# Two normalising multiplies of layer 0 on GpSimd, a third temporary in the back, and the first half's delta loads tied to one store

## The chip, the cores and the metric

The program runs on one core of one Trainium2 chip. The metric is the device time of one execution in microseconds (us), lower is better. The engines are called as in the profile: PE (TensorE), PEld (its weight loads), DVE (VectorE), ACT (ScalarE), POOL (GpSimd) and SP (SyncE, which issues the DMAs).

## The reference

Two layers act on an image of 2 x 96 x 96 x 96 (batch, channels, rows, columns). All of the change lies in layer 0. Cut to what matters:

```
x = x + L0_conv(_ln_c(x))          # _ln_c: norm over the channels, eps 1e-6
t = tokens(x);  t = t + L0_ffn(_ln_t(t));  x = image(t)
...layer 1...

def L0_conv(x):
    xin, z = split(in_proj(x));  z = silu(z)
    x_s = grid_sample_bilinear(xin, ref + offset(xin))      # 3x3 conv, norm, gelu, 1x1 conv, tanh
    # 512 windows of 6 x 6 tokens, 4 directions, 192 channels, 16 states
    delta = softplus(dt_proj(x_proj(x_s)) + bias)
    h[t] = h[t-1] * exp(delta * A) + delta * u * B[t]
    y[t] = sum over the 16 states of h[t] * C[t], plus D * u
    y = sum of the four directions
    y = (y - mean(y)) * rsqrt(var(y) + 1e-5) * ln_g + ln_b   # over the 192 channels
    return out_proj(y * z)
```

## The kernel before

Layer 0 walks 32 stripes (2 images x 16 stripes of 6 rows, T = 576 tokens, H2 = 288). A stripe has three parts, and the parts of neighbouring stripes overlap.

**Front** (`_l0_front`, L488). It norms x over the channels (`norm`, L532), projects, gates, convolves, samples bilinearly on POOL (`sample`, L675, 14 multiplies and adds), and for the two token orders o = 0, 1 computes B, C, delta and delta*u (`steps`, L781: four POOL operations in each of three channel groups m). The last step stores delta and delta*u in DRAM (`dl_d`, `du_d`; `store`, L825). Group m = 0 holds channels 0 to 127 of direction kk = 0, group m = 1 the same of kk = 1, and m = 2 the last 64 channels of both. In `norm`, ACT writes the square into `asq` and the centred value into `axc`; PE averages the square into PSUM tile `ava`; ACT makes it a reciprocal root in place (Ln, then Exp with -0.5, L548 and L549); DVE multiplies (L552). No GpSimd instruction of this kernel touches PSUM.

**Scan** (`_l0_scan`, `_l0_section`, L1055). A stripe has 64 units: half h of the channels (0, 1), order o, direction kk, quarter i of the states, half c of the tokens, in this nesting. A unit is: PE spreads B over 128 rows of PSUM (L1104, `bp`, two buffers), DVE multiplies by delta*u (L1108), ACT makes the decays (L1088, `dA`), DVE scans (L1125, result in one of six `h` buffers), POOL multiplies by C (L1130), PE adds up the states in PSUM tile `y` (L1143). The delta rows `dlr` and `dur` of a section (h, o, kk) come by one DMA each (L1073), two buffers each; before the change such a load is planned behind every store of its direction, m and m = 2. After 32 units ACT copies `y` into `Y` (L1039, L1041), of which there is one buffer.

**Back** (`_l0_back`, L936). It centres Y, norms it (`normed`, L971: PE averages the squares into `yva`, ACT makes the reciprocal root in PSUM, `_power`, L857; DVE multiplies both halves of Y, L975), multiplies by the gate z on POOL (L984), projects and adds the input (`pp`, L994 to L1001), and runs the feed-forward net (`_plan_ffn`). Its temporaries `ysq`, `ysq2`, `fxc`, `fsq` and `x2` share the buffers of tag "b", two before the change.

The order of the work is not written by hand. `_Plan` records every operation of all 32 stripes with its engine, a cost and a due time; `order` is a list scheduler that walks engines and buffers through these numbers, picks for each engine the operation that can start first, then the one due first, and takes a buffer only when one is free. What it gives is issued, and `_in_order` then fixes it: each of PE, DVE, ACT, POOL and SP executes its instructions in exactly that order. A cost that is a little longer or an edge less therefore gives another order everywhere. POOL's costs are 0.14 us + 0.0018 us a column (1.7 us for L1130). `keep` puts matmuls without use (L1188, on `minus`) where the plan leaves PE idle. A tile's `skip` leaves that many words free at its start.

Of the kernel before, what the change touches and what calls it, by code (L numbers as in the profile page):

```python
# [13 lines left out]
AF = mybir.ActivationFunctionType  # L14
ALU = mybir.AluOpType
# [11 lines left out]
C = 96  # L27
HW = 96
# [4 lines left out]
T = WIN * HW  # L33
H2 = T // 2
NS = 16
KG = 4
NQ = 4
CB = 32
NBL = C // CB
# [69 lines left out]
class _Plan:  # L109
# [19 lines left out]
    def op(self, eng, cost, run, r=(), w=(), due=0.0, tab=None, also=(), scan=False, first=False):  # L129
        o = _Op(eng, cost * self.rate.get(eng, 1.0), run, due, tab)  # L130
        o.scan, o.first = scan, first
        ref = lambda t: t if isinstance(t, tuple) else (t, None)
        meets = lambda a, b: a is None or b is None or a == b
        for t, key in map(ref, r):
            o.deps.update(p for p, q in t.writes if meets(key, q))
        for t, key in map(ref, w):
            o.deps.update(p for p, q in t.writes + t.reads if meets(key, q))
        for t, key in map(ref, r):
            t.reads.append((o, key))
        for t, key in map(ref, w):  # L140
            t.writes.append((o, key))
        o.deps.discard(o)
        for t in [x[0] for x in map(ref, list(r) + list(w))] + list(also):
            if t not in o.tiles:
                o.tiles.append(t)
        for t in o.tiles:
            if not t.users and t.tag != "p":
                t.queue.append(t)
            t.users.append(o)
        self.ops.append(o)  # L150
        return o
# [323 lines left out]
def _cost(S, eng, cols):  # L475

    fixed, each = (RATE if S.fine else LOOSE)[eng]
    return fixed + each * cols


def _op(S):
    def op(eng, n, run, r, w, also=(), tab=None, times=1):
        S.op(eng, times * _cost(S, eng, n), run, r, w, also=also, tab=tab)

    return op


def _l0_front(k, P, S, f, x, b, s, at):  # L488
# [3 lines left out]
    nc = k.nc  # L492
# [4 lines left out]
    temp = lambda shape, name, skip=0: S.tile(P.front, shape, "g", P.ng, name=name, skip=skip)  # L497
# [4 lines left out]
    def pe(cols, run, r, w, also=()):  # L502
        S.op("pe", _cost(S, "pe", cols), run, r, w, also=also)

    def act(cols, run, r, w, tab=None, times=1):
        S.op("act", times * _cost(S, "act", cols), run, r, w, tab=tab)

    def dve(cols, run, r, w):
        S.op("dve", _cost(S, "dve", cols), run, r, w)
# [17 lines left out]
    pool(8, lambda: nc.gpsimd.memset(xin.ap[:, :, :, 1 : HW + 3 : HW + 1], 0.0), (), (xin,))  # L527
    rows = lambda t, c: t.ap[:, 4 * c : 4 * c + 4, :].rearrange("p r w -> p (r w)")
    N4 = 4 * HW
    xc, sq, xn = temp([C, 8, HW], "axc"), temp([C, 8, HW], "asq"), temp([C, 8, HW], "xn")  # L530

    def norm(c):  # L532
        pc, va = ps("axc"), ps("ava")
        pe(N4, lambda: nc.tensor.matmul(
            pc.ap[:C, :N4], k.less_mean, rows(xt, c), start=True, stop=True), (xt,), (pc,), (xc,))

        def centred():
            nc.scalar.activation(rows(sq, c), pc.ap[:C, :N4], AF.Square)
            nc.scalar.copy(rows(xc, c), pc.ap[:C, :N4])

        act(N4, centred, (pc,), ((xc, c), (sq, c)), times=2)
        pe(N4, lambda: nc.tensor.matmul(
            va.ap[:C, :N4], k.mean96, rows(sq, c), start=True, stop=True),
            ((sq, c),), (va,), (xn,))

        def power():
            v = va.ap[:C, :N4]
            nc.scalar.activation(v, v, AF.Ln, bias=k.eps6[:C])  # L548
            nc.scalar.activation(v, v, AF.Exp, scale=-0.5)  # L549

        act(N4, power, (), (va,), tab="e", times=2)
        dve(N4, lambda: nc.vector.tensor_tensor(  # L552
            rows(xn, c), rows(xc, c), va.ap[:C, :N4], ALU.mult), ((xc, c), va), ((xn, c),))

    def project(half, c):
        pi, n = ps("pi"), PART[half]
# [7 lines left out]
    for c in range(2):  # L564
        norm(c)
# [26 lines left out]
    t = temp([128, NBL, H2], "t")  # L592
# [255 lines left out]
def _dues(S, n0, at):  # L848

    ops = S.ops[n0:]  # L850
    whole, sofar = sum(o.cost for o in ops), 0.0
    for o in ops:
        o.due = at(sofar / whole)
        sofar += o.cost


def _power(k, op, v, eps, out=None):  # L857

    v_ = lambda: v.ap[:C, :H2]

    def run():
        k.nc.scalar.activation(v_(), v_(), AF.Ln, bias=eps[:C])
        k.nc.scalar.activation(v_() if out is None else out.ap, v_(), AF.Exp, scale=-0.5)

    op("act", H2, run, (), (v,) if out is None else (v, out), tab="e", times=2)
# [70 lines left out]
def _l0_back(k, P, S, f, ffn, res, dst, at):  # L936

    nc = k.nc
    n0 = len(S.ops)
    Y, zs = f.Y, f.zs  # L940
    temp = lambda name: S.tile(P.back, [C, T], "b", 2, name=name)
    ps = lambda name: S.tile(P.ps, [128, 512], "p", P.np, name=name)
    cols = lambda c: slice(c * H2, (c + 1) * H2)

    op = _op(S)
    xr = S.tile(P.back, [C, T], "xr", 1)
    S.op("sp", 1.2, lambda: nc.sync.dma_start(
        xr.ap.rearrange("p (i w) -> p i w", w=HW), res), (), (xr,))
    x1, sq = xr, [temp("ysq"), temp("ysq2")]

    def both(w, src, name, r):

        out = ps(name)

        for half in range(2):
            op("pe", H2, lambda half=half: nc.tensor.matmul(
                out.ap[:C, :H2], w(half), src(half), start=(half == 0), stop=(half == 1)),
                r, (out,))
        return out

    def centred(c):
        pc = [both(lambda half, h=h: k.less_mean192 if half == h else k.minus_mean192,
                   lambda half: Y.ap[:, half, cols(c)], "yc", ((Y, c),)) for h in range(2)]
        for h in range(2):
            def run(h=h):
                nc.scalar.activation(sq[h].ap[:, cols(c)], pc[h].ap[:C, :H2], AF.Square)
                nc.scalar.copy(Y.ap[:, h, cols(c)], pc[h].ap[:C, :H2])

            op("act", H2, run, (pc[h],), ((sq[h], c), (Y, c)), times=2)

    def normed(c):  # L971
        va = both(lambda half: k.mean192, lambda half: sq[half].ap[:, cols(c)], "yva",
                  ((sq[0], c), (sq[1], c)))
        _power(k, op, va, k.eps5)
        op("dve", 2 * H2, lambda: nc.vector.tensor_tensor(  # L975
            Y.ap[:, :, cols(c)], Y.ap[:, :, cols(c)],
            va.ap[:C, :H2].unsqueeze(1).to_broadcast([C, 2, H2]), ALU.mult),
            (va,), ((Y, c),))

    for c in range(2):  # L980
        centred(c)
        normed(c)
    for h in range(2):
        op("pool", T, lambda h=h: nc.gpsimd.tensor_tensor(  # L984
            Y.ap[:, h], Y.ap[:, h], zs.ap[:, h], ALU.mult), (zs,), (Y,))

    def project(c):
        pp = ps("pp")

        half = slice(c * HW // 2, (c + 1) * HW // 2)  # L990
        img = lambda t: t.ap.rearrange("p (i w) -> p i w", w=HW)[:, :, half].rearrange(
            "p i (w j) -> p w i j", j=WIN)

        op("pe", H2, lambda: nc.tensor.matmul(  # L994
            pp.ap[:C, :H2], k.ident[:C, :C], img(x1), start=True, stop=False), (Y, zs, (x1, c)), (pp,))
        for n, (w, v) in enumerate(((k.w_outb, zs), (k.w_out, Y))):
            for h in range(2):
                op("pe", H2, lambda n=n, w=w, v=v, h=h: nc.tensor.matmul(
                    pp.ap[:C, :H2], w[:, h, :], v.ap[:, h, cols(c)],
                    start=False, stop=(n == 1 and h == 1)), (v,), (pp,))  # L1000
        op("act", H2, lambda: nc.scalar.copy(  # L1001
            img(x1), pp.ap[:C, :H2].rearrange("p (w i j) -> p w i j", i=WIN, j=WIN)),
            (pp,), ((x1, c),))

    for c in range(2):
        project(c)

    x2 = _plan_ffn(k, S, op, ps, temp, P.back, 1, ffn, x1)
    S.op("sp", 1.2, lambda: nc.sync.dma_start(dst, x2.ap), (x2,), ())
    _dues(S, n0, at)  # L1010
# [44 lines left out]
def _l0_section(k, P, S, f, first, o, h, kk, py, at, tau):  # L1055


    nc = k.nc
# [12 lines left out]
    for name, d in (("dlr", f.dl[kg]), ("dur", f.du[kg])):  # L1071
        t = S.tile(P.rep, [128, NBL, T], name, 2)
        S.op("sp", 2.6, lambda t=t, d=d: nc.sync.dma_start(  # L1073
            t.ap.rearrange("p b t -> p (b t)"),
            d.ap[:, 3 * h : 3 * h + 3, :].rearrange("c b t -> c (b t)").unsqueeze(1)
            .to_broadcast([CB, NQ, NBL * T])), (d,), (t,), due=at - 9 * tau)
        reps.append(t)
    dlr, dur = reps

# [961 lines left out]
```

## Time and profile before

| what | value |
|---|---|
| median of 3 runs (lowest, highest) | 8276.61 us (8267.24, 8282.14) |
| the profiled execution, and its span from first to last instruction | 8276.3 us, 8274.5 us |
| granted TensorE clock, mean | 0.959 |
| first scan starts, last scan ends | 149.4 us, 6227 us |
| busy between these two, of 6077.6 us: DVE, PE, POOL, ACT | 5896.2, 5297.0, 5019.1, 4695.2 us |
| L552, DVE: count, mean | 64, 532 ns |
| L975, DVE: count, mean | 64, 732 ns |
| L984, POOL, the nearest operation to those that move: count, mean | 64, 1203 ns |

A group of the profile is one line of code on one engine: busy time, mean length of one, then the time the engine sat idle just before such an instruction and who ended that idle time. A length runs from start to end of one instruction; neighbours on DVE overlap by a little, so spacing from start to start is shorter. The chain of work that ended last is the page's own account of the critical path; for this program it holds 28% of the span, so windows and waits say more.

### The profile page before, as it was taken

What the parts mean: (1) busy time and instruction counts of PE and PEld (TensorE: products, weight loads), DVE (VectorE), ACT (ScalarE), POOL (GpSimd) and SP (SyncE); (2) the same over time, 40 slices, a digit from 0 to 9 for tenths busy, and PEclk for the clock granted to TensorE, in tenths of its full rate; (3) what the DMA queues carried; (4) which work ended last, traced back from release to release, by engine and by line L of the source; (5) the groups of instructions that cost most, each with busy time, mean ns of one, the idle gap of its engine ahead of it and who ended that gap; (6) DMA issues with size and microseconds to landing.
All of it is one profiled execution on the core that took longest, in us unless ns stands there. A gap on an engine that the chain in (4) does not pass through costs nothing. (4 is left out here: it accounts for less than half of the span.)

```text
span 8274.5 us, 124621 instructions
## 1 busy us (share of the span) xinstructions
PE 7337.5 (89%) x46413; PEld 3261.5 (39%) x46413; DVE 7653.1 (92%) x5404; ACT 6308.6 (76%) x10654; POOL 5188.3 (63%) x3835
## 2 busy tenths in 40 slices
PE   7888888888888888888888888988878999989998
PEld 3333344434334333434443433433334223532245
DVE  3999999999999999999999999999996998969988
ACT  5777777778777887877777787778756886778867
POOL 4888888888888888888888888888862000110001
PEclk8999998999999999999999999999999999989999
DMA  3445544544545454454545454454441000110001
GB/s 93 159 156 156 157 151 155 156 151 156 157 153 158 156 166 153 153 159 155 155 150 157 150 157 156 155 159 158 154 132 47 3 3 20 33 47 3 2 22 33
DMA packets 359853, 992.25 MB, mean 120 GB/s; under 512 B 69288, under 2 KB 71680, under 8 KB 359040
## 3 DMA queue, kind: packets, MB, share of 16 engines
q1 hardware_dynamic: 357440, 984.04, 38.3%
q8 instruction: 367, 6.01, 0.3%
q14 instruction: 254, 2.08, 0.1%
q10 hardware_dynamic: 1792, 0.12, 0.0%
HBM read 797.19 MB, written 139.25 MB: 113 GB/s over the span
## 5 line engine op out<-in xcount | busy, mean ns | idle before, releaser
L1130 POOL TENSOR_TENSOR h<-h,cre 128x864 f32<-128x864 f32 x2048 | 3475.2, 1713 | 957.4 <-DVE h L1125 639.7
L1125 DVE TENSOR_TENSOR_SCAN h<-dA,bp 128x864 f32<-128x864 f32 x2048 | 3900.6, 1939 | 51.2 <-PE y L1143 30.6
L1088 ACT ACTIVATE dA<-dlr,A 128x576 f32<-128x576 f32 x3072 | 2157.9, 765 | 892.8 <-DVE h L1125 839.8
L1108 DVE TENSOR_TENSOR bp<-dur,bp 128x864 f32<-128x864 f32 x2048 | 2082.2, 1048 | 187.9 <-PE bp L1104 81.4
L1143 PE MATMUL y<-h,fold 128*32 128x288 f32 (+2 forms) x18432 | 1789.7, 436 | 229.6 <-POOL h L1130 202.1
L1143 PEld LDWEIGHTS y<-h,fold 128*32 128x32 f32 x18432 | 738.8, 114 | 963.4 <-POOL h L1130 674.8
L1503 ACT ACTIVATE pr<-sc 128x960 f32<-128x960 f32 (+1 forms) x1080 | 954.0, 937 | 200.1 <-PE sc L1499 179.2
L1104 PE MATMUL bp<-bt,selb 128*128 128x288 bf16 x2048 | 615.6, 301 | 508.4 <-DVE h L1125 491.2
L1583 DVE TENSOR_TENSOR sums<-sums,pr 128x3840 f32<-128x3840 f32 (+1 forms) x240 | 959.1, 3996 | 55.7 <-ACT pr L1503 33.7
L1675 POOL MEMSET vch<- 96x32 f32 x16 | 2.4, 153 | 1319.7 <-DVE dist L1537 1210.1
L1104 PEld LDWEIGHTS <-selb 128*128 128x128 bf16 x2048 | 198.9, 97 | 1200.9 <-DVE h L1125 1006.3
L1499 PE MATMUL sc<-qH,kH 32*128 32x480 f32 (+1 forms) x3240 | 627.4, 602 | 9.6 <-issue 5.0
L1188 PE MATMUL y<-selb,minus 128*32 128x288 bf16 x3528 | 605.7, 295 | 0.0
L1499 PE MATMUL sc<-q,kH 32*128 32x480 f32 (+1 forms) x1080 | 564.6, 602 | 0.0
L1565 PE MATMUL av<-pr,vT 128*32 128x480 f32 (+1 forms) x4320 | 533.4, 564 | 3.7 <-ACT av L1590 3.5
L1756 DVE SCALAR_TENSOR_TENSOR acc<-vch,lepe_w,acc 96x1152 f32<-96x1152 f32 x320 | 466.2, 1457 | 8.4 <-ACT vch L1691 0.4
L1188 PEld LDWEIGHTS <-minus 128*32 128x32 bf16 x3528 | 298.0, 98 | 225.6 <-issue 131.2
L1499 PEld LDWEIGHTS sc<-qH,kH 32*128 32x128 f32 x3240 | 219.6, 184 | 419.8 <-issue 220.6
L617 PE MATMUL pc<-xin,w_ca 128*128 128x288 f32 x1152 | 365.1, 423 | 1.2 <-ACT xin L560 1.2
L932 POOL TENSOR_TENSOR x<-x,fy 96x576 f32<-96x576 f32 x32 | 52.9, 1653 | 461.4 <-ACT fy L931 372.4
L791 PE MATMUL pt<-xd,w_dt 96*128 96x288 f32 x768 | 280.7, 455 | 7.3 <-ACT r L797 4.4
L810 POOL TENSOR_TENSOR e<-e,du 128x576 f32<-128x576 f32 x192 | 231.1, 1204 | 60.0 <-ACT du L806 59.7
(284 smaller groups left out, 10961.8 us busy)
## 6 DMA issues: line engine op xcount, KB each, us to landing
cre<-c_d SPq DMA_DIRECT2D x1024, 288.0 KB, 3.5
dur<-du_d SPq DMA_DIRECT2D x256, 864.0 KB, 5.6
dlr<-dl_d SPq DMA_DIRECT2D x256, 864.0 KB, 5.1
x<-xs SPq DMA_DIRECT2D x512, 72.0 KB, 2.4
du_d<-du SPq DMA_DIRECT2D x128, 288.0 KB, 2.5
dl_d<-dl SPq DMA_DIRECT2D x128, 288.0 KB, 2.6
du_d<-du SPq DMA_DIRECT2D x128, 144.0 KB, 2.5
dl_d<-dl SPq DMA_DIRECT2D x128, 144.0 KB, 2.4
```

The lines of the kernel that those rows point to most:

```text
L1088: nc.scalar.activation(dA.ap[:, :, blk, :], dlr.ap[:, blk, :].rearrange("p (c n) -> p c n", c=2), AF.Exp, scale=k.A[:, i, kg, h, blk : blk ...
L1104: nc.tensor.matmul(bp.ap[:, :H2], k.selb[:, kk, i, :], f.bc[o].ap[:, toks], start=True, stop=True)
L1108: nc.vector.tensor_tensor(bp.ap[:, : NBL * H2].rearrange("p (b n) -> p b n", b=NBL)[:, ::-1], dur.ap[:, ::-1, toks], bp.ap[:, :H2].unsquee ...
L1125: nc.vector.tensor_tensor_scan(hv, dv, bv, 0.0, ALU.mult, ALU.add)
L1130: nc.gpsimd.tensor_tensor(ht.ap, ht.ap, cre.ap[:, toks].unsqueeze(1).to_broadcast([128, NBL, H2]), ALU.mult)
L1143: nc.tensor.matmul(dst, k.fold, v, start=start, stop=stop)
L1188: nc.tensor.matmul(P.awake.ap[NBL * CB :, T - HEAD + 2 * 72 : HEAD], k.minus[:, :CB], k.selb[:, 0].rearrange("p i m -> p (i m)")[:, : HEAD ...
L1499: nc.tensor.matmul(two[to // 2][:, to % 2, :n], kH[rows, k0 : k0 + 128], q, start=True, stop=True)
L1503: nc.scalar.activation(pr[:, 2 * i : 2 * i + 2, :n], two[i][:, :, :n], AF.Exp, scale=HD**-0.5)
L1565: nc.tensor.matmul((main if s < HEADS else other)[s * HD : (s + 1) * HD, :n], vT[:, blk, hd, :], pr[:, place(s, p), :n], start=at == 0, st ...
L1583: nc.vector.tensor_tensor(both, both, pr[:, :, :, :n], ALU.add)
L1756: S.op("dve", 1.43, lambda: nc.vector.scalar_tensor_tensor(acc.ap, src(), W.lw[:, t : t + 1], acc.ap, ALU.mult, ALU.add), (vch,), (acc,))
```

## The change

Three edits, all in layer 0.

1. In the front's `norm` and in the back's `normed`, the reciprocal root is written by ACT into an SBUF tile (the tile of the squares, `asq` or `ysq`, which is free by then), and the multiply is POOL's and not DVE's. `asq` gets a skip of two words.
2. The back's shared temporaries get three buffers and not two, with a skip of two words.
3. For h = 0, the plan lets a load of `dlr` or `dur` follow the store of group m = kk alone. For h = 1 it stays behind all stores of its direction.

```diff
@@ _l0_front, norm
-    xc, sq, xn = temp([C, 8, HW], "axc"), temp([C, 8, HW], "asq"), temp([C, 8, HW], "xn")
+    xc, sq, xn = temp([C, 8, HW], "axc"), temp([C, 8, HW], "asq", 2), temp([C, 8, HW], "xn")
...
-            nc.scalar.activation(v, v, AF.Exp, scale=-0.5)
-
-        act(N4, power, (), (va,), tab="e", times=2)
-        dve(N4, lambda: nc.vector.tensor_tensor(
-            rows(xn, c), rows(xc, c), va.ap[:C, :N4], ALU.mult), ((xc, c), va), ((xn, c),))
+            nc.scalar.activation(rows(sq, c), v, AF.Exp, scale=-0.5)
+
+        act(N4, power, (), (va, (sq, c)), tab="e", times=2)
+        pool(N4, lambda: nc.gpsimd.tensor_tensor(
+            rows(xn, c), rows(xc, c), rows(sq, c), ALU.mult), ((xc, c), (sq, c)), ((xn, c),))
@@ _l0_back
-    temp = lambda name: S.tile(P.back, [C, T], "b", 2, name=name)
+    temp = lambda name: S.tile(P.back, [C, T], "b", 3, name=name, skip=2)
...
-        _power(k, op, va, k.eps5)
-        op("dve", 2 * H2, lambda: nc.vector.tensor_tensor(
+        rs = lambda: sq[0].ap[:, cols(c)]
+
+        def power():
+            nc.scalar.activation(va.ap[:C, :H2], va.ap[:C, :H2], AF.Ln, bias=k.eps5[:C])
+            nc.scalar.activation(rs(), va.ap[:C, :H2], AF.Exp, scale=-0.5)
+
+        op("act", H2, power, (), (va, (sq[0], c)), tab="e", times=2)
+        op("pool", 2 * H2, lambda: nc.gpsimd.tensor_tensor(
             Y.ap[:, :, cols(c)], Y.ap[:, :, cols(c)],
-            va.ap[:C, :H2].unsqueeze(1).to_broadcast([C, 2, H2]), ALU.mult),
-            (va,), ((Y, c),))
+            rs().unsqueeze(1).to_broadcast([C, 2, H2]), ALU.mult),
+            ((sq[0], c),), ((Y, c),))
@@ _l0_section, loads of dlr and dur
-            .to_broadcast([CB, NQ, NBL * T])), (d,), (t,), due=at - 9 * tau)
+            .to_broadcast([CB, NQ, NBL * T])), ((d, kk),) if h == 0 else (d,), (t,), due=at - 9 * tau)
```

In the built program every line after the second edit stands six lines lower (the scan L1125 becomes L1131, POOL's L1130 becomes L1136, the gate multiply L984 becomes L990, the loads L1073 become L1079); L552 keeps its number on its new engine, and L975 becomes L981.

## The prediction, made before the changed kernel ran

> **What bounds the kernel now.** I read the page's busy times and slices first, then the windows, then groups, waits and timelines of the part that is changed.
>
> ```profile
> PE 7337.5 (89%) x46413; PEld 3261.5 (39%) x46413; DVE 7653.1 (92%) x5404; ACT 6308.6 (76%) x10654; POOL 5188.3 (63%) x3835
> ...
> DVE  3999999999999999999999999999996998969988
> ...
> 149.40:6227.00 6077.60, 5297.01 (x34106) 2420.16 (x34105) 5896.23 (x4278) 4695.24 (x8118) 5019.07 (x3605) 0.96 0.49 154
> ```
>
> POOL works only in layer 0, so its 63% says little. The window (columns PE, PEld, DVE, ACT, POOL) runs from the first scan to the last: DVE is busy 5896.2 of 6077.6 us (97%), POOL 83%. DVE bounds this stage and stands idle for 181 us of it.
>
> ```profile
> 6204.37 2.03 DVE L1108 TENSOR_TENSOR bp<-dur,bp 128x864 f32<-128x864 f32 x2
> 6206.28 3.81 DVE L1125 TENSOR_TENSOR_SCAN h<-dA,bp 128x864 f32<-128x864 f32 x2
> 6209.99 2.03 DVE L1108 TENSOR_TENSOR bp<-dur,bp 128x864 f32<-128x864 f32 x2
> ```
>
> Undisturbed, two units take 6209.99 - 6204.37 = 5.62 us: each instruction costs less than its length, since neighbours overlap. So I price by spacing.
>
> ```profile
> L975 DVE TENSOR_TENSOR Y<-Y,yva 96x576 f32<-96x576 f32 x64 | 46.9, 732 | 10.2 <-ACT yva L863 10.2
> L552 DVE TENSOR_TENSOR xn<-axc,ava 96x384 f32<-96x384 f32 x64 | 33.8, 532 | 65.4 <-ACT ava L549 65.4
> ...
> DVE bp L1108 <- PE bp L1104: 81.4, 106, 2.6
> DVE h L1125 <- PE y L1143: 30.6, 26, 4.7
> DVE bp L1108 <- POOL h L1130: 27.8, 40, 1.9
> ```
>
> The last three are DVE's largest waits of the stage (total, times, longest): for PE's spread, and, twice over, for an `h` buffer that POOL or PE has not given back. Before the first scan it waits most:
>
> ```profile
> 133.43 1.37 SPq L1073 DMA_DIRECT2D dur<-du_d x2
> ...
> 147.22 4.10 ACT L1088 ACTIVATE dA<-dlr,A 128x576 f32<-128x576 f32 x6
> ...
> 138.80 2.03 DVE L1108 TENSOR_TENSOR bp<-dur,bp 128x864 f32<-128x864 f32 x2 [50.05 <-DMA dur<-du_d]
> 149.36 3.80 DVE L1125 TENSOR_TENSOR_SCAN h<-dA,bp 128x864 f32<-128x864 f32 x2 [8.54 <-ACT dA L1088]
> ```
>
> The first `dur` load leaves at 133.4 us, although group m = 0 was stored at 110.4; the stores of m = 2 (127.1 to 129.6) stand ahead of it.
>
> **What the Trainium skill says.** "GPSIMD Engine Reference", section 3.1, gives about 2.6 cycles an element for a two-input operation at 1.2 GHz: 1248 ns for 576 elements; the trace has L984 at 1203 and spacings of 1.28 us, so it agrees. "SBUF — State Buffer", section "Who interferes with whom", lets GpSimd and a DVE instruction with two SBUF inputs block each other. The stage's products and scans take one input from PSUM, and POOL's L1130 stays within 1702 and 1734 ns beside them: no block, here or for the two new operations. "ScalarE: Activation LUTs", section "Step-by-step: what each stage is for", calls PSUM the quicker destination: this trace has 387 ns for an Exp into PSUM (L863, `fva`) and 407 into SBUF (`frs`). "DMA: Bandwidth & Descriptors", section "Anatomy of one DMA", puts some 2 us of completion on a DMA; the stores here land 2.5 us after issue.
>
> **The change, part by part.** The sum is made against the profiled execution, 8276.3 us (span 8274.5); the median, 8276.61, is the same to 0.3 us, so nothing is shifted.
>
> *DVE gives up its multiplies.* L552: spacing 2001.55 to 2002.01 = 0.46 us, 60 of 64 within the stage (four come before the first scan): 27.6. L975: 1168.70 to 1169.35 = 0.65 us, 62 within (the last stripe's two come after the last scan): 40.3. Together **-67.9 us** on the engine that bounds the stage.
>
> *POOL takes them.* Neither is in the trace. From 576 to 864 columns the rows L984 and L1130 rise by 1713 - 1203 = 510 ns, 1.77 ns a column; so 384 columns take 1203 - 192 x 1.77 = 863 ns. Low end 0.80 (in proportion), high end 1.10 (in proportion to layer 1's slow L932, mean 1.65 us). L981, 576 columns: 1.28 by spacing, ends 1.20 and 1.65. I take 0.86 and 1.28: 2 x 0.86 + 2 x 1.28 = 4.3 us a stripe, 137 in all (128 to 176), queued ahead of L1130. POOL goes from 5019 to some 5155 of a stage of about 6020, 86%: cost nothing directly, hidden behind DVE's scans; uncovered it costs up to the 137.
>
> *Waits that grow.* (a) For `h` buffers, 30.6 + 27.8 = 58.4 us: priced over both built orders, POOL's other work between the h multiplies rises from 53.6 to 57.9 us a stripe, 8%; its longest run, 13 operations or 16.7 us, is the same, and there are 30 runs above 15 us in both. 8% of 58.4 is +5. (b) A moved multiply also gave PE half a microsecond more for the next spread. 106 of 1024 pairs of products wait for it, so 122 x 0.10 x 0.55 = +7. Together **+12**; ends -40 (the new order waits less) and +60.
>
> *The start.* In the changed order SP issues the loads of `dur` and `dlr` right after the m = 0 stores and one `c_d` store (112.9 in this trace). The wait for the store's landing holds SP to about 113.5; behind it stand the m = 1 stores (ready 115.5) and four `x` loads, which lose nothing. With 5.6 us to landing, `dur` is there at 119. Next late is ACT: its first decays stand behind the Relu of the next delta step (ends 126.3) and two `xin` copies, whose matmuls end at 128.1. So decays from 128.6, three of them 2.1 us, first scan at 130.8 instead of 149.4: -18.6. Two first norms on POOL add 0.3: **-18.3**. The next loads keep pace: kk = 1 is due 8 units (23 us) later and its store leaves soon after 115.6; POOL's steps for o = 1 now stand after 2, 6 and 10 h multiplies, needed at unit 16. Stripe 1's last delta step stands after 54 h multiplies (49 before), needed at 64. Later stripes have no DMA wait to lose: the start's is the only large one.
>
> *Edits with one answer.* Exp into SBUF: +20 ns x 128 = 2.6 us on ACT, 77% busy, so 0. Third buffer and skips: `ysq` is held until POOL has multiplied, the third buffer pays for that; no row waits on these tiles, 0. The last stripe's Y multiply: 1.20 for 0.73, **+0.5**. Layer 1: 0.
>
> Sum: 8276.3 - 67.9 - 18.3 + 12 + 0.5 = **8202.6**.
>
> **The rivals.**
>
> *POOL runs behind its plan and stops PE (the slow side).* PE executes in the planned order, and the plan prices POOL too low: 1.18 for 576 columns against 1.28, 1.70 for L1130 against 3.50 / 2 = 1.75. New waits stand in PE's queue: `pi` (L557) for xn, and `pp` for Y, which has to be out before unit 32 of the next stripe, when ACT copies into the one `Y`. A stopped PE holds the spreads queued behind it. For: PE already waited 198 us for POOL's h (401 times); the longest DVE wait, 4.7 us, is at such a handover. Against: POOL in turn waited for DVE's scan 345 times, 594.6 us, so it catches up; and Z (L990) stands at unit 22 to 30 of the next stripe, as before (16 to 30). It decides from (67.9 + 18.3 - 0.5) / 32 = 2.7 us a stripe, and beyond 3.2 the kernel is slower by more than 0.2%. If all 137 us arrive: 8276.3 - 85.7 + 137 = **8328**. Chance 7%.
>
> *Half of DVE's time turns into waits.* For: spread waits come after every tenth pair and nothing speeds up PE (87% busy). Against: 97% of the stage is DVE's work. 8202.6 + 34 = **8237**. Chance 20%.
>
> *The new order waits less.* For: it repeats nearly the same from stripe to stripe (Z at 22 or 27 in 28 of 32), and PSUM tiles `ava` and `yva` are free after ACT. Against: the moved work lands on POOL, whose lag causes a third of the waits. Some 35 us less: **8168**. Chance 18%.
>
> *The start doesn't move* (the load is early, but PE or ACT holds the first scan): 8202.6 + 18.3 = **8221**. Chance 8%.
>
> **How the numbers follow.** My forecast 47%, the others as given. Time 8202.6; range 8160 to 8255, from the waits' ends (-40 and +60 against +12 give 8151 and 8251) and the middle rivals, leaving out most of the slow one. A difference of 0.2% (16.6 us) is about what a measurement of this kernel can tell from no change. Slower: 6 of the slow rival's 7%. Same: its last 1% and the worst 5% of the half rival. Faster: the rest, 88%.
>
> **What would show it.** Right: no DVE row for L552 and L981, POOL rows of 64 at 0.8 to 0.9 and 1.2 us; first scan near 131; DVE idle in the stage near 190 us; stage length near 6022. Wrong: first scan after 140; DVE waits for PE's spread or y, or for POOL's h, up by more than 60 us together; `pi` or `pp` waiting for POOL by microseconds a stripe; L1130 spread beyond 1734 ns.

## The result, and the profile after

| kernel | median, us (lowest to highest, runs) | ratio to before, 95% interval |
|---|---|---|
| before | 8272.03 (8267.24 to 8282.14, 4) | 1 |
| after | 8169.05 (8157.44 to 8174.17, 4) | 0.9872 (0.9855 to 0.9889) |

The changed kernel is 103 us faster, 34 us below the forecast and inside its range. The profiled executions stand 109.9 us apart: 8166.36 us (span 8164.6) after, 8276.3 before.

From the page of after: the busy times and DVE's slices.

```profile
PE 7220.7 (88%) x46243; PEld 3227.6 (40%) x46243; DVE 7585.0 (93%) x5276; ACT 6359.5 (78%) x10684; POOL 5311.4 (65%) x3963
...
DVE  4999999999999999999999999999996998869988
```

The window of after from the first scan to the last (busy PE, PEld, DVE, ACT, POOL, then clock, DMA share, GB/s):

```profile
131.80:6117.80 5986.00, 5203.62 (x33994) 2400.91 (x33992) 5830.13 (x4156) 4760.67 (x8173) 5145.79 (x3737) 0.98 0.49 157
```

Against before's 6077.60 us with DVE busy 5896.23, this divides the 109.9 us: the first scan comes 17.6 us earlier (149.4 to 131.8), DVE is busy 66.1 us less, DVE idle falls by 25.5 (181.4 to 155.9), and what follows the last scan is 0.7 shorter. The idle time had been forecast to rise by 12.

The moved multiplies, from the groups of after by line:

```profile
L981 POOL TENSOR_TENSOR Y<-Y,ysq 96x576 f32<-96x576 f32 x64 | 77.0, 1204 | 8.4 <-ACT ysq L978 8.4
...
L552 POOL TENSOR_TENSOR xn<-axc,asq 96x384 f32<-96x384 f32 x64 | 55.3, 865 | 33.3 <-ACT asq L549 27.3 <-issue 5.9
```

They are POOL's now: 0.865 us, as priced, and 1.204 us, which the prediction had as a length but priced by its spacing, 1.28. In the stage POOL is busy 126.7 us more (5019.1 to 5145.8), where 137 had been priced. The timeline of the start after:

```profile
111.55 0.60 SPq L828 DMA_DIRECT2D du_d<-du  x1
114.40 0.56 SPq L1079 DMA_DIRECT2D dur<-du_d  x1
...
119.69 2.02 DVE L1114 TENSOR_TENSOR bp<-dur,bp 128x864 f32<-128x864 f32 x2 [98.60 <-DMA dur<-du_d]
129.66 4.11 ACT L1094 ACTIVATE dA<-dlr,A 128x576 f32<-128x576 f32 x6
131.79 1.95 DVE L1131 TENSOR_TENSOR_SCAN h<-dA,bp 128x864 f32<-128x864 f32 x1 [10.08 <-ACT dA L1094]
```

The load leaves at 114.4 and not at 133.4; the first product gains 19.1 us, and then, as forecast, ACT is late: its decays start at 129.66 (forecast 128.6) and the scan waits 10.08 us for them. DVE's waits in the stage after (total, times, longest; the 10.1 of the last row is the wait before the first scan):

```profile
DVE h L1131 <- PE y L1149: 76.9, 39, 9.0
DVE bp L1114 <- PE bp L1110: 25.4, 48, 1.9
DVE bp L1114 <- POOL h L1136: 21.7, 45, 1.7
DVE h L1131 <- ACT dA L1094: 12.8, 8, 10.1
```

Here two movements cancel, and more. Waits for the return of an `h` buffer (first and third row) rose from 58.4 to 98.6 us; waits for PE's spread fell from 81.4 to 25.4. The first row has two shapes. Most of it comes once a stripe, as in this stretch of POOL's timeline after:

```profile
3911.90 5.05 POOL L1136 TENSOR_TENSOR h<-h,cre 128x864 f32<-128x864 f32 x3
3916.91 1.20 POOL L682 TENSOR_TENSOR top<-dif,fr 128x576 f32<-128x576 f32 x1
...
3931.76 1.20 POOL L687 TENSOR_TENSOR bot<-bot,fr 64x576 f32<-64x576 f32 x1
3932.92 5.06 POOL L1136 TENSOR_TENSOR h<-h,cre 128x864 f32<-128x864 f32 x3
```

and what DVE did then:

```profile
3935.48 3.80 DVE L1131 TENSOR_TENSOR_SCAN h<-dA,bp 128x864 f32<-128x864 f32 x2 [1.78 <-PE y L1149]
```

Thirteen operations of other work keep POOL from `h` for 16.0 us, 5.7 units at 2.81 us. By this reading six buffers, of which one is being written and others are still being summed, don't quite cover that, and DVE waits 1.78 us. After's steady part has 25 such bursts of 13 operations and 5 of 12; before has 10 of 13 and 20 of 12 (counted in the POOL order of the two traces, memsets left out). The other shape is the single wait of 9 us:

```profile
1189.44 0.56 ACT L1045 COPY Y<-y 96x504 f32<-96x504 f32 x1
1190.01 0.66 ACT L1047 COPY Y<-y 32x72 f32<-32x72 f32 x3
...
1190.82 2.85 PE L1149 MATMUL y<-h,fold 128*32 128x288 f32 x29 [2.38 <-ACT Y L1047]
...
1192.08 1.95 DVE L1131 TENSOR_TENSOR_SCAN h<-dA,bp 128x864 f32<-128x864 f32 x1 [8.96 <-PE y L1149]
```

ACT may copy `y` into the one `Y` only when the stripe before has let go of it; until then PE's sums stop, and then DVE. In after's built order that stripe's second gate multiply (L990) stands behind 30 h multiplies of the next stripe, close to unit 32. All other stripes of the steady part have it at 22 to 27, and none of them has such a wait. This is the prediction's slow rival, at the place it named, once.

### The profile page after: what moved, and what is told of

Same layout as the page of the kernel before. It is cut to its first block, busy times and chain, and to the rows that moved or that the text cites. A ratio compares the mean times of both kernels' runs of the same rounds, so it can differ in the third digit from the quotient of the medians.

```text
span 8164.6 us, 124255 instructions
## 1 busy us (share of the span) xinstructions
PE 7220.7 (88%) x46243; PEld 3227.6 (40%) x46243; DVE 7585.0 (93%) x5276; ACT 6359.5 (78%) x10684; POOL 5311.4 (65%) x3963
## 5 line engine op out<-in xcount | busy, mean ns | idle before, releaser
L1131 DVE TENSOR_TENSOR_SCAN h<-dA,bp 128x864 f32<-128x864 f32 x2048 | 3902.8, 1939 | 103.3 <-PE y L1149 76.9
L1136 POOL TENSOR_TENSOR h<-h,cre 128x864 f32<-128x864 f32 x2048 | 3474.9, 1714 | 768.3 <-DVE h L1131 547.0
L1114 DVE TENSOR_TENSOR bp<-dur,bp 128x864 f32<-128x864 f32 x2048 | 2073.3, 1046 | 161.2 <-DMA dur<-du_d 98.6
L1149 PE MATMUL y<-h,fold 128*32 128x288 f32 (+2 forms) x18432 | 1760.1, 432 | 228.0 <-POOL h L1136 212.2
L1194 PE MATMUL y<-selb,minus 128*32 128x288 bf16 x3358 | 575.7, 295 | 0.0
L1194 PEld LDWEIGHTS <-minus 128*32 128x32 bf16 x3358 | 278.5, 98 | 217.9 <-issue 128.8
L796 ACT ACTIVATE e<-pt,dt_b 128x288 f32<-128x288 f32 x384 | 191.2, 498 | 94.2 <-PE pt L791 70.1
```

What stands on the lines that cost most here:

```text
L1114: nc.vector.tensor_tensor(bp.ap[:, : NBL * H2].rearrange("p (b n) -> p b n", b=NBL)[:, ::-1], dur.ap[:, ::-1, toks], bp.ap[:, :H2].unsquee ...
L1131: nc.vector.tensor_tensor_scan(hv, dv, bv, 0.0, ALU.mult, ALU.add)
L1136: nc.gpsimd.tensor_tensor(ht.ap, ht.ap, cre.ap[:, toks].unsqueeze(1).to_broadcast([128, NBL, H2]), ALU.mult)
L1149: nc.tensor.matmul(dst, k.fold, v, start=start, stop=stop)
L1194: nc.tensor.matmul(P.awake.ap[NBL * CB :, T - HEAD + 2 * 72 : HEAD], k.minus[:, :CB], k.selb[:, 0].rearrange("p i m -> p (i m)")[:, : HEAD ...
```

## The experiments

Theories as the experiments began: the edits themselves lower the waits, because PSUM tiles are free sooner once ACT writes the root into SBUF (P), or because of the third temporary (T); or the order of the work lowers them, whatever the edits do (O); or the plan's low POOL prices are what costs, and truer ones would gain (C). The table gathers all runs; no kernel leaves work out, and where work is added it is named below. "Gate" is where the built order puts a stripe's second gate multiply, in h multiplies of the next stripe (the last two stripes are left out). DVE's busy and idle time are of the stage. The ratios are each to before on the same chip, whose medians lay between 8272 and 8277 us.

| kernel | median, us | ratio to before (95%) | first scan | DVE busy | DVE idle | gate |
|---|---|---|---|---|---|---|
| before | 8272.03 | 1 | 149.4 | 5896.2 | 181.4 | 16 to 30 |
| after | 8169.05 | 0.9872 (0.9855 to 0.9889) | 131.8 | 5830.1 | 155.9 | 22 to 30 |
| loads_only | 8297.02 | 1.0029 (1.0019 to 1.0039) | 129.3 | 5907.6 | 215.0 | 18 to 29 |
| norms_only | 8253.20 | 0.9974 (0.9966 to 0.9983) | 144.1 | 5833.1 | 222.4 | 15 to 35 |
| temps_only | 8292.72 | 1.0020 (1.0012 to 1.0028) | 152.1 | 5887.4 | 216.4 | 16 to 26, mostly 21 |
| norms_temps | 8154.60 | 0.9853 (0.9830 to 0.9877) | 144.1 | 5822.8 | 138.7 | 15 to 27, mostly 27 |
| dve_gets_back | 8214.10 | 0.9930 (0.9918 to 0.9943) | 133.3 | 5896.3 | 143.0 | as after |
| pool_twice | 8239.41 | 0.9959 (0.9945 to 0.9972) | 132.9 | 5837.9 | 229.9 | as after |
| pool_costs | 8470.93 | 1.0237 (1.0221 to 1.0253) | 133.3 | 5823.0 | 467.5 | 21 to 27, 34 |
| h7_b2 | 8250.59 | 0.9971 (0.9962 to 0.9981) | 131.9 | 5834.1 | 216.5 | 23 to 35 |
| costs_early | 8207.79 | 0.9922 (0.9908 to 0.9935) | 132.4 | 5837.5 | 186.5 | 19 |
| after_early | 8164.86 | 0.9869 (0.9854 to 0.9884) | 131.9 | 5830.7 | 155.5 | 19 |
| before_early | 8194.13 | 0.9908 (0.9893 to 0.9923) | 150.0 | 5887.9 | 113.0 | 15, 16 |
| norms_temps_early | 8178.52 | 0.9883 (0.9868 to 0.9898) | 149.9 | 5829.0 | 160.2 | 19, once 15 |

### The edits one by one: loads_only, norms_only, temps_only, norms_temps

Each is the kernel before with one edit of the change alone; norms_temps has edits 1 and 2, so it is after without the third:

```diff
@@ norms_temps, against after
-            .to_broadcast([CB, NQ, NBL * T])), ((d, kk),) if h == 0 else (d,), (t,), due=at - 9 * tau)
+            .to_broadcast([CB, NQ, NBL * T])), (d,), (t,), due=at - 9 * tau)
```

> The kernel before with the third edit alone (for h = 0 a load of dlr or dur follows the store of group m = kk only). Theory S (what the parts were priced at): the first scan moves from 149.4 to about 131.8 us and the rest of the stage keeps its waits, so 8272 - 18 = 8254 us. Rival O (any edit gives another order everywhere, and that alone moves the waits by some 30 us either way): the start moves by the same 18 us, but DVE's idle time in the scan stage lies anywhere from 150 to 210 us and the time from 8224 to 8284 us.

> The kernel before with the first edit alone: roots into SBUF, both multiplies on POOL, two shared temporaries, loads as before. Theory P (the waits for PE's spread fell because the PSUM tiles of the two norms are given back after ACT and DVE's place in the order is gone): DVE's busy time falls by 66 us and its waits for the spread from 81 to about 25 us, so 8272 - 66 - 25 = 8181 us. Theory S with the waits as first priced: 8272 - 68 + 12 = 8216 us. Rival T (the third temporary did it): with two of them the squares are held until POOL has multiplied, the feed-forward part comes late, waits grow and the time is at 8216 us or above.

> The kernel before with the second edit alone: three shared temporaries in the back and a skip of two words. Theory P: nothing waits on these tiles before, so within 10 us of 8272 us. Rival T: the order of the back gets freer, DVE's waits for the spread fall to 25 to 50 us, and the time to about 8245 us. Rival O: up to 30 us either way, with no wait that names the back.

> The changed kernel without its third edit. Theory S: only the start is given back, first scan at about 149 us, 8169 + 18 = 8187 us, waits of the stage as in the changed kernel (about 155 us of idle DVE). Rival O: the start is given back and the stage's idle time is anywhere from 130 to 200 us, so 8160 to 8235 us.

Measured, against before's 8276.77 of the same chip: +20, -24, +16, and -122 for the first two edits together. They don't add: the three alone sum to some +13, all three give -103. loads_only is slower and norms_temps faster than any of their expectations had it. The direct effects are there every time: both kernels with edit 1 have DVE busy 5823 to 5833 us, both without it 5887 to 5908, and the loads alone start the scans at 129.3. The start isn't the third edit's alone, though: both kernels with edit 1 and without edit 3 start at 144.1, 5.3 us ahead of the kernel before. What differs without a pattern is the idle time, 139 to 222 us. The loads' 20 us at the start are eaten by 34 us more idle and 11 us more busy time further on. temps_only, whose gate stands at 21 in 28 stripes, idles 216 us; so regularity alone isn't what helps. norms_only has two hand-overs at 35 and two waits of 20.3 us, the longest below:

```profile
DVE h L1131 <- PE y L1149: 88.5, 36, 20.3
DVE bp L1114 <- PE bp L1110: 55.7, 89, 3.4
```

The fastest of all runs is norms_temps, from its window:

```profile
144.10:6105.60 5961.50, 5236.23 (x33725) 2380.07 (x33723) 5822.77 (x4156) 4710.87 (x8136) 5126.57 (x3727) 0.97 0.50 157
```

It starts 12.3 us later than after, and its stage is 24.5 us shorter. The interval of its ratio overlaps that of after, so it isn't shown to be faster; but no gain of the third edit is shown on top of the other two.

### The two prices in one order: dve_gets_back and pool_twice

Both have after's built order with 128 useless instructions added behind the moved multiplies; nothing is left out.

```diff
@@ dve_gets_back, behind the multiply of norm (of normed: T columns)
+            nc.vector.tensor_reduce(k.taken, k.some[:, :N4], AX.X, ALU.max)
@@ pool_twice, behind the multiply of norm (of normed: 512 columns)
+            nc.gpsimd.tensor_tensor(k.taken[:, :N4], k.some[:, :N4], k.some[:, 2 : N4 + 2], ALU.mult)
```

> The changed kernel with the order of every engine kept as it is, and at the place of each of the 128 moved multiplies one more DVE instruction without use: a reduction of 384 or 576 columns of a constant tile to one value that nobody reads. It takes about as long as L552 and L975 did. Nothing is planned for it, so the order of all other instructions stays. Theory S (DVE's own time is what the stage pays): slower by 122 x 0.46 to 0.65 us = 55 to 75 us, so about 8169 + 66 = 8235 us. Rival: part of the moved time would have stood in a wait anyway, slower by 30 us or less, 8199 us.

> The changed kernel with its order kept and each of the 128 multiplies on POOL followed by one more without use, of 384 and 512 columns, on constant tiles: 64 x 0.86 + 64 x 1.17 = some 130 us more on POOL. Theory S (POOL's part is hidden behind DVE's scans): at most 20 us slower, 8170 to 8190 us, through more waits for h buffers. Rival B (POOL's queue sets the pace by now, through PE's queue behind it): slower by half of it or more, 8235 us and above.

The windows of the two, dve_gets_back first:

```profile
133.30:6172.60 6039.30, 5245.71 (x33994) 2421.44 (x33992) 5896.27 (x4279) 4756.06 (x8174) 5143.24 (x3737) 0.96 0.50 156
132.90:6200.70 6067.80, 5280.19 (x33994) 2435.34 (x33992) 5837.86 (x4156) 4756.69 (x8173) 5252.42 (x3859) 0.96 0.49 155
```

dve_gets_back: DVE busy 66.1 us more, 13 us less idle, the stage 53.3 longer, the median up by 45. So 0.7 (by the medians) to 0.8 (by the stages) of what DVE does more arrives in the time; its waits take up a part. pool_twice: POOL busy 106.6 us more in the stage (5145.8 to 5252.4), the stage 81.8 longer, DVE idle 74.1 more, the median up by 70. This second dose of POOL work isn't hidden behind the scans: 0.7 to 0.8 us of each microsecond arrived. What the first dose, the moved multiplies themselves, costs is not measured by it. One way that it takes shows in DVE's waits of pool_twice,

```profile
DVE h L1137 <- PE y L1155: 72.0, 43, 2.9
DVE bp L1120 <- PE bp L1116: 66.1, 99, 2.5
DVE bp L1120 <- POOL h L1142: 40.0, 45, 1.5
```

and in PE's, here of after:

```profile
PE bp L1110 <- DVE h L1131: 502.2, 892, 2.0
PE y L1149 <- POOL h L1136: 212.2, 397, 1.5
```

and of pool_twice:

```profile
PE bp L1116 <- DVE h L1137: 441.7, 761, 2.0
PE y L1155 <- POOL h L1142: 284.6, 431, 2.2
```

PE waits 72 us more for POOL's h; behind those sums stand the next spreads in PE's queue, and DVE's waits for a spread rise from 25.4 to 66.1. So a wait that names PE can be POOL's. A second way isn't excluded: the granted clock of the stage fell from 0.98 to 0.96, and the same 33994 matmuls kept PE busy for 5280.2 us, not 5203.6. In dve_gets_back the clock is at 0.96 too and PE busy 5245.7, with 28.2 us of waits for a spread; so the lower clock alone doesn't make them, but how the rise divides is open.

### Truer POOL prices, and another buffer: pool_costs and h7_b2

pool_costs plans after with POOL's spacings as the prediction read them (1.28 us for 576 columns; the burst above has 1.23 in the mean), and nothing else; h7_b2 gives the third temporary's space to a seventh `h` buffer.

```diff
@@ pool_costs
-RATE = {... "pool": (0.14, 0.0018), ...}
+RATE = {... "pool": (0.33, 0.00165), ...}
-        S.op("pool", 1.7, times_c, ...)
+        S.op("pool", 1.755, times_c, ...)
@@ h7_b2
-    temp = lambda name: S.tile(P.back, [C, T], "b", 3, name=name, skip=2)
+    temp = lambda name: S.tile(P.back, [C, T], "b", 2, name=name, skip=2)
-        P.np, P.ng, P.nda, P.nh = 3, 5, 2, 6
+        P.np, P.ng, P.nda, P.nh = 3, 5, 2, 7
```

> The changed kernel planned with POOL's costs as the trace spaces them: 0.33 us + 0.00165 us a column in place of 0.14 + 0.0018, and 1.755 us for the multiply by C in place of 1.7. Theory C (the waits that are left come from a plan that thinks POOL earlier than it is): PE's waits for POOL's h (209 us) and DVE's for y (77 us) fall, DVE idle from 155 to about 110 us, 8169 - 45 = 8124 us. Rival O: another order with other waits, within 30 us of 8169 us.

> The changed kernel with seven h buffers in place of six, and two shared temporaries in place of three to make room for the seventh. If DVE's waits for y and for POOL's h (77 + 22 us) come from bursts of POOL's other work that outrun six buffers, one more buffer is worth 2.8 us in each of the 32 bursts: most of the 77 us go, 8169 - 60 = 8109 us. If they come from PE's queue standing still, the buffers change little: 8150 to 8180 us. If the third temporary matters, it is slower than that by what norms_only is slower than norms_temps less the start.

pool_costs is the slowest kernel of all, 302 us behind after. DVE's waits over the whole of it begin

```profile
DVE h L1131 <- PE y L1149: 360.4, 44, 21.8
```

and the timeline shows what they are made of, one for every stripe from 3326 to 5979 us:

```profile
3326.33 3.80 DVE L1131 TENSOR_TENSOR_SCAN h<-dA,bp 128x864 f32<-128x864 f32 x2 [17.48 <-PE y L1149]
3531.93 3.80 DVE L1131 TENSOR_TENSOR_SCAN h<-dA,bp 128x864 f32<-128x864 f32 x2 [21.85 <-PE y L1149]
3737.00 3.80 DVE L1131 TENSOR_TENSOR_SCAN h<-dA,bp 128x864 f32<-128x864 f32 x2 [19.57 <-PE y L1149]
```

There are 16 such waits of 16.7 to 21.9 us, 309 us in all, and 16 stripes in the built order whose gate multiply stands behind 34 h multiplies, past unit 32. (The expectation of costs_early below counts 19 stripes; the trace's order has 16.) Elsewhere the gate is at 27 or less, and no wait for these sums is longer than 3.6 us. The 16 waits are as much as the whole gap: the loss is the hand-over of `Y`. Two units late cost more than two units of time because more follows the gate: in the first wait shown, the second gate multiply starts at 3310.0, the last projection that reads `Y` (L1004) ends at 3324.1, ACT copies at 3324.3, and PE takes up its sums at 3325.6.

h7_b2 has the same thing three times (32, 35, 35: waits of 10.0, 17.6 and 17.6 us) and waits of 76.2 us for the spread. What the seventh buffer is worth in time can't be read from it, since the temporaries and the order changed too; three temporaries and seven buffers together were not run. At the bursts it can be read. The same 13 operations in 16.0 to 16.1 us come 11 times in h7_b2; DVE's wait for PE's sums just behind them is 0 to 1.1 us there, where the 25 of after have 1.8 to 2.9. The longest of the 11 (its burst ends at 3610.08):

```profile
3612.94 1.95 DVE L1131 TENSOR_TENSOR_SCAN h<-dA,bp 128x864 f32<-128x864 f32 x1 [1.08 <-PE y L1149]
```

That bears out the reading of the bursts.

### Due times eight units earlier: costs_early, after_early, before_early, norms_temps_early

One number moves the back's work ahead of unit 32 in the plan, without touching what is computed or by which engine (ACT's table loads and the plan's filler matmuls follow the order, though, and change in number):

```diff
-            t0, t1 = (64 * n + 68) * tau, (64 * n + 135) * tau
+            t0, t1 = (64 * n + 60) * tau, (64 * n + 127) * tau
```

It is applied to pool_costs, after, before and norms_temps.

> pool_costs with one edit more: the back's due times 8 units earlier, which puts the gate multiply at 19 h multiplies after the stripe's end in every stripe, where pool_costs had 34 in 19 stripes. Theory H (a gate multiply planned close to unit 32 or behind it holds up the hand-over of the single Y buffer, and DVE stops there for 16 to 22 us): the 15 to 20 us waits for y, 289 us in the 15 longest plus what leads to them, are gone, no wait for y above 4 us is left, and the time is within 40 us of the changed kernel, 8130 to 8210 us. Rival (truer costs for POOL are bad for the order in other ways): it stays above 8300 us.

> The changed kernel with the back's due times 8 units earlier; gate multiplies at 19 in every stripe, the one at 30 is gone. Theory H: its single wait of 9 us goes, 8169 - 9 = 8160 us, and what else the other order does to the waits is seen beside it. Theory O (waits depend on the whole order): within 30 us of that either way.

> The kernel before with the back's due times 8 units earlier (gate multiplies at 15 or 16; in before they stood at 16 to 30). No multiply is moved. Theory O: the changed kernel's waits fell by 25 us because its order had no late gate multiplies and repeats from stripe to stripe; then this kernel, with such an order, also gains some 25 us, 8276 - 25 = 8251 us, and the difference to after_early is what the moved work and the start are worth, 66 + 18 = 84 us. Rival P (giving PSUM back early lowers the waits): no gain here, 8276 us, and 110 us or more to after_early.

> norms_temps (no third edit) with the back's due times 8 units earlier. Its order in the later stripes is nearly that of after_early. Theory S: with like orders the third edit is worth what it moves the first scan by, 12 to 18 us, so this kernel is 12 to 18 us slower than after_early, about 8175 us. Rival: the third edit's gain at the start is lost again in the first stripes, and the two are within 8 us of each other.

costs_early is 263 us faster than pool_costs: with the gate at 19, no wait in the stage for PE's sums is longer than 2.6 us.

```profile
DVE h L1131 <- PE y L1149: 89.3, 51, 2.6
```

That confirms the hand-over from the other side. It is still 43 us slower than after_early, so these truer prices don't give a better order here (C falls).

The largest surprise is before_early: the same work, 81 us faster than before by its order alone, where the expectations had 25 us or nothing. (In the stage it has 72 ACT instructions less, all of them table loads, and 279 matmuls less, all of them fillers.) DVE's largest waits in its stage:

```profile
DVE bp L1108 <- PE bp L1104: 43.1, 63, 2.2
DVE bp L1108 <- POOL h L1130: 38.3, 63, 1.1
DVE bp L1108 <- PE y L1143: 18.6, 17, 1.2
```

and in that of after_early:

```profile
DVE h L1131 <- PE y L1149: 51.8, 40, 2.4
DVE bp L1114 <- POOL h L1136: 28.3, 57, 1.4
DVE bp L1114 <- PE bp L1110: 24.2, 37, 1.8
```

Between before and before_early the waits for an h buffer hardly move (58.4 to 56.9); those for the spread fall from 81.4 to 43.1, and the rest of the idle time from 41.6 to 13.0.

With like due times the change is worth 29 us (8194.13 to 8164.86; the runs are 8192.0 to 8205.4 and 8160.7 to 8172.2). The windows of the two say how:

```profile
150.00:6150.90 6000.90, 5288.91 (x33827) 2406.64 (x33826) 5887.89 (x4278) 4584.37 (x8046) 5014.65 (x3605) 0.96 0.51 156
131.90:6118.10 5986.20, 5261.82 (x34105) 2423.58 (x34102) 5830.69 (x4156) 4645.98 (x8105) 5147.66 (x3737) 0.98 0.51 157
```

First scan 18.1 us earlier, DVE busy 57.2 less, but idle 42.5 more, so the stage is shortened by only 14.7; what follows the last scan is 6.8 longer. POOL is busy 133.0 more, and the h buffers' waits rise (18.6 + 38.3 to 51.8 + 28.3), which fits it. Put against each other, 42.5 of 133.0 is about a third; that is an estimate for the moved multiplies, since the orders still differ.

Earlier due times don't help every kernel: norms_temps_early is 24 us slower than norms_temps by the medians (their intervals just overlap). The 29 us are the change's worth in one pair of orders, not its worth as such. norms_temps_early against after_early prices the third edit where the gate stands alike: 13.7 us in the medians, with the first scan at 149.9 against 131.9; the two intervals of the ratios overlap, so the traces carry this more than the times.

## Why the prediction was right, and where its sum was not

*DVE gives up its multiplies, -67.9.* Right: -66.1. But a busy microsecond isn't a microsecond of time; put back in the same order, 66.1 us cost 45.

*POOL takes them, hidden, 0.* The lengths were right (865 and 1204 ns). "Hidden behind DVE's scans", at no cost, was wrong as a rule: a second dose of such work arrives by 0.7 to 0.8 in after's order (pool_twice), and for the moved multiplies themselves the pair with like due times gives about a third. So the truth lies between the 0 of the sum and the 137 us of the bound. The error didn't show in the total, since another covered it.

*Waits that grow, +12.* This is the term that failed: measured -25.5. Step (a), +5 for `h` buffers, was too small; these waits grew by 40.2. It took the bursts for unchanged ("30 runs above 15 us in both"), and at 1.28 us an operation 12 of them count as above 15 us as well as 13. But bursts of 13 rose from 10 to 25, and in after the waits just behind those 25 come to some 60 us of the 98.6. Step (b), +7 because a moved multiply had given PE half a microsecond more, had the wrong sign: the spread's waits fell by 56.0, and dve_gets_back, which gives DVE those half microseconds back in the same order, has 28.2 us of them, no fewer than after's 25.4 (at a lower clock, 0.96 for 0.98). The rest of the idle time fell by some 10. The rival "the new order waits less" (8168) named the outcome to a microsecond, though not its parts.

*What filled the gap: the order.* From before to before_early only the order changes, and 81 us go, of them 68 us of DVE's idle time. From there to after_early the edits bring 29. From there to after, the medians differ by 4, which is within their spread. So most of the 103 us could be had without any of the three edits: the kernel before stood in a poor order, and the edits changed it. What waits the new order would have was not worked out rightly beforehand, even in sign, so that the total came this near is in part luck. The waits' ends in the prediction (-40 to +60) were the right kind of caution, and they kept the result inside the range, 9 us above its lower end.

*The start, -18.3.* Right: -17.6, and by the steps named (load at once behind the first group's stores, then ACT late), though 5.3 us of it come without the third edit in norms_temps, where the prediction had the first norms on POOL cost 0.3. As a gain it holds only with the rest of the order: alone the edit loses 20 us; on top of the first two it gains nothing that is shown with the old due times, and 13.7 us with the earlier ones.

*POOL runs behind its plan.* As a stop at every hand-over it did not come true, since the gate stands at 22 to 27 in nearly all stripes; as a mechanism it is shown in four kernels (9 us once in after, 20.3 twice in norms_only, 10.0 to 17.6 in h7_b2, 309 in pool_costs). A gate before 30 is no guarantee: loads_only has a wait of 7.8 us at a hand-over whose gate stood at 26, since there the projection behind the gate came late on PE. PE's other new waits did not show: among PE's waits of after's stage none of `pi` or `pp` is for POOL, and `pp` waited twice after the last scan, 2.8 us together. The sign that L1130 would spread beyond 1734 ns did come, by 5 ns (1739).

*Half of DVE's time turns into waits.* Near the truth for the edits apart from the order: 42.5 of 57.2 in the pair with like due times. It lost as a forecast only because the order gave more back.

*Open.* What makes one order wait less for the spread than another isn't settled, and 38 of the 68 us of idle time that before_early saves lie there. Kernels with edit 1 have 24 to 40 us of it where the gate comes in time (pool_twice apart), those without it 43 to 81, so P may have a part; but before_early has the least idle time of all, 113.0 us, with the roots still in PSUM, so P isn't needed. T explains little alone (temps_only +16), yet norms_only without it has the late gates and norms_temps with it none. The granted clock alone isn't the cause: 0.98 in after's stage and 0.96 in before's, but also 0.96 in before_early, and in dve_gets_back with 28 us of spread waits. It moves with the time all the same: of before's 51 executions on one chip the one at 0.964 took 8248.01 us and one at 0.954 took 8297.25, 4.9 us for each thousandth. From before to after the mean rose by 7 thousandths (0.959 over those 51 to 0.966 over after's 4), which at that rate would be some 34 of the 103 us, an estimate. Whether the clock lengthens the waits or PE's waits lower the clock, no run here shows.

## What to carry to other kernels

Where a planner makes the order, an edit's worth is its price plus a new order, and the second can be the larger: shift one due time in both kernels and compare again before crediting the edit, and take even that for one pair of orders. Work moved to an engine that is 83% busy and works in bursts isn't hidden merely because another engine bounds the stage; price it through the buffers and the queue that it holds. Look for the last user of every single buffer, and keep it in the plan well ahead of the unit in which the buffer is written again: two units too late cost 17 to 22 us a stripe here.

## What the runs showed of the hardware

The Trainium skill, "SBUF — State Buffer", section "Who interferes with whom", has a DVE operation with at most one SBUF input, outside the two-port modes, leave GpSimd alone. The runs agree, also for operations that were new here: POOL's L1136 kept to 1702 to 1739 ns after (1702 to 1734 before), and to 1701 to 1735 with 128 DVE reductions of one SBUF tile added. The block itself, with two SBUF inputs, no run here shows.

POOL's lengths here fit a fixed part and a share for each column, not a share alone: 865 ns for 384 columns, 1204 for 576 and 1714 for 864, which is 1.77 ns a column and some 185 ns beside. The 2.6 cycles an element that the prediction takes from "GPSIMD Engine Reference", section 3.1, give by its reckoning 1248 ns for 576 columns and 1872 for 864, as estimates; the first fits, the second is 9% above the measured 1714. In the burst shown above the starts lie 1.16 to 1.29 us apart, 1.23 in the mean (16.0 / 13), and the plan has 1.18. Planning with 1.28 still made the order worse.
